# Deformable layer: the y offsets of two rows of taps are laid on all lanes by transfers, and three batches of tents are made per row of blocks

## The chip, the cores and the metric

The kernel runs on one core of a Trainium2 chip. The metric is the device time of one execution in microseconds; three runs of the kernel before gave 5567.96, 5574.5 and 5575.89 us, so the median is 5574.5 us. The core has five engines with a queue each, worked off in order: PE (matrix products; PEld is its loading of weights), DVE (elementwise and reductions), ACT (activations and copies), POOL and SP, which here only issues transfers. The transfers themselves run on 16 DMA engines.

## The reference, cut to what matters

Four layers follow one another on x of shape (4, 128, 128, 128), each with a group normalisation ahead of it and a residual sum behind it. The change touches only the first, a deformable 3x3 convolution:

```
offset = einsum('bchw,oc->bohw', x, w_off) + b_off          # 72 maps: 4 groups x 9 taps x {dy, dx}
py = dy + (ky - 1) + row ;  px = dx + (kx - 1) + column     # for each of the 9 taps (ky, kx)
y0, x0 = floor(py), floor(px)
val  = x[y0, x0]     * (1 - wy) * (1 - wx) + x[y0, x0 + 1]     * (1 - wy) * wx
     + x[y0 + 1, x0] * wy       * (1 - wx) + x[y0 + 1, x0 + 1] * wy       * wx
out  = relu(einsum('bgckhw,ogck->bohw', val, w_def))        # 9 taps x 128 channels -> 128 channels
x    = x + out
```

`wy` and `wx` are the fractions of py and px, and the 32 channels of a group share their offsets. A bilinear weight is a tent: max(0, 1 - |py - y|) * max(0, 1 - |px - x|) for each pixel (y, x).

## The kernel before

The layer is `deform_layer`. It assumes that no offset is larger than 1 (a flag `far` sends other inputs to `deform_general`), so that what a block of 3 rows by 4 columns of outputs needs lies in a window of 5 by 6 pixels. The 30 pixels of the window for each of 4 groups make 120 lanes (`LANES`). A sample is then a matrix product: the pixels of the window (`pixels`, 120 lanes x 128 channels, one such matrix for each of 33 column blocks) times the tents `m` (120 lanes x 27 x 4 columns), where a lane holds the weight of its own pixel for each of 9 taps and 3 rows.

The tents are made in three steps. `load_places` fetches the offsets of three rows of outputs (a "row of blocks") from DRAM (`offs`), where each offset is split into three bf16 parts and their positive parts (`parts`, 6 rows in each of 4 groups; with a row of ones that makes `KROWS` = 25). `spread_offsets` (line 498) multiplies them on PE with a constant table `spread`, which lays on each lane 1 - |offset - distance| in its row and clips it where the distance needs it. For one tap that takes three products for y (one per row, 130 columns) and four for x (one per column phase, 3 x 33 columns). Products of 25 rows use a quarter of the array each; two taps with y and x stand in the four quarters (partitions 0, 32, 64, 96) and are issued in turn. `tents` copies the y part out of PSUM on ACT (`ty`, line 508) and multiplies it with the x part on DVE (line 510). The PSUM tile `t_ps` has two buffers of two banks.

`sample` (line 521) multiplies pixels and tents for four column blocks, `keep_samples` (lines 531, 536) copies the result from PSUM to `v` on ACT, `convolved` (line 579) multiplies `v` with the weights of the 9 taps, and `finish` (line 552) adds the residual on DVE.

The order on each engine is the order of the code (`manual_schedule`). The main loop runs over 172 rows of blocks (43 in each of 4 images) and, inside, over `NG_X` = 8 groups of column blocks. In group i of row n it issues: the spreads of taps of row n + 1 that `DONE` asks for, the copy of the last group's samples, a piece of the convolution of row n - 1, the samples of group i, the tents of the spreads, up to six statistics of finished outputs (`count`), and one or two steps of the preparation of later rows (`step`). Five lists of taps (`SLOTS`, four pairs and a single) are spread per row, in groups 0, 2, 3, 5 and 6. `load_pixels` for row n + 1 is issued at the start of row n, `load_row` (which calls `load_places`) for row n + 2 in group 3.

Preparation is either `counted` (statistics of an image, 16 rows a chunk, for the group normalisation) or `prepared` (16 rows a job, four rows at a time): PE transposes (line 370), ACT scales (line 373), SP stores the pixel table; PE multiplies with `w_off` (line 385), DVE and POOL scale and shift it (lines 390, 393), ACT, POOL and DVE make the bf16 parts (lines 409 to 418) and the ranges for `far` (lines 412, 414), and SP stores the parts every eight rows (line 423). It keeps some 26 rows ahead of the samples.

In the last row of blocks of an image (`end`) a further output row is made with three extra tents (`me`) and samples (`ve`).

Of the kernel before, what the change touches and what calls it, by code (L numbers as in the profile page):

```python
# [49 lines left out]
SLOTS = [(0, 6), (1, 7), (2, 8), (3, 5), (4,)]  # L50
# [130 lines left out]
def deform_layer(tc, c, small, x, w_off, b_off, w_def, x1, tabs, offs):  # L181
# [13 lines left out]
    NB = RY * PADW  # L195
    with ExitStack() as ctx:
        wp = ctx.enter_context(tc.tile_pool(name="l0w", bufs=1))
        ps_g = ctx.enter_context(tc.tile_pool(name="l0ps_g", bufs=1, space=PSUM))
        ps_t = ctx.enter_context(tc.tile_pool(name="l0ps_t", bufs=2, space=PSUM))
# [4 lines left out]
        NPH = NPY + NPX  # L204
        keep = ctx.enter_context(tc.tile_pool(name="l0keep", bufs=2))
# [9 lines left out]
        places = [wp.tile([P, len(SLOTS), RY, OW], BF16, name=f"places_{i}") for i in range(3)]  # L215
        last = wp.tile([P, 3, 1, OW], BF16, name="places_last")
        pixels = [wp.tile([P, NXB + 1, P], F32, name=f"pixels_{i}") for i in range(2)]
        parts = wp.tile([2 * NL, NPART, 2 * RO * OW], BF16, name="parts")

        def rims():  # L220

            zero = two.tile([P, 2 * SX * P], F32, name="zero", tag="m")
            nc.vector.memset(zero, 0.0)
            zrow = zero[0 : NXB + 1]
            zoff = zero[0 : 2 * NL, 0 : NPART * OW].bitcast(BF16)
            zoff = zoff.rearrange("p (n l) -> p n l", n=NPART)
            for b in range(B):
# [14 lines left out]
                nc.scalar.dma_start(rows_[:, :, (S + 2) * OW :], zoff)  # L242

        def tables():

            awayi = two.tile([NG, NPH, LANES], I32, name="awayi", tag="x1c")
# [22 lines left out]
            for i, sign in enumerate((-1.0, 1.0, 1.0)):  # L269
                nc.gpsimd.memset(picks[:, i], sign)  # L270
# [17 lines left out]
            for t in (*pixels, parts):  # L288
                nc.gpsimd.memset(t, 0.0)
            yield  # L290
            picks16 = one.tile([NG, 3, P], BF16, name="picks16", tag="ve")
            nc.vector.tensor_copy(picks16, picks.rearrange("g k q r -> g k (q r)"))
            kinds = two.tile([NG, 3, NPH * LANES], BF16, name="kinds", tag="m")
# [10 lines left out]
            n = NPH * LANES // 3  # L304
            for h in range(3):
                if h % 2 == 0:
                    tp = ps_t.tile([P, 2, 512], F32, name="t_ps")
                at = slice(h * n, (h + 1) * n)
                for i in range(3):
                    nc.tensor.matmul(  # L310
                        tp[:, h % 2, 0:n], lhsT=picks16[:, i], rhs=kinds[:, i, at],
                        start=i == 0, stop=i == 2,
                    )
                nc.scalar.copy(to[:, at], tp[:, h % 2, 0:n])
# [43 lines left out]
        def prepared(b, y0):  # L358
# [6 lines left out]
            for h in range(0, RC, RO):  # L365
# [23 lines left out]
                off = one.tile([2 * NL, RO, S], F32, name="off")  # L389
# [8 lines left out]
                p0 = h % (2 * RO)  # L398
                at = slice(p0 * OW, (p0 + RO) * OW)

                def to(i):
                    return parts[:, i, at].rearrange("p (r c) -> p r c", c=OW)[:, :, 2 : S + 2]

                def high(t):
                    halves = t.rearrange("p r c -> p (r c)").bitcast(BF16)
                    return halves.rearrange("p (r c two) -> p r c two", r=RO, two=2)[:, :, :, 1]

                rest = one.tile([2 * NL, RO, S], F32, name="rest")
                nc.scalar.copy(to(0), high(off))
                nc.gpsimd.tensor_tensor(rest, off, high(off), ALU.subtract)  # L410
                flat = off.rearrange("p r c -> p (r c)")
                nc.vector.tensor_reduce(ranges[:, 0, n : n + 1], flat, AX.X, ALU.max)
                yield
                nc.vector.tensor_reduce(ranges[:, 1, n : n + 1], flat, AX.X, ALU.min)
                nc.scalar.copy(to(1), high(rest))
                nc.gpsimd.tensor_tensor(to(2), rest, high(rest), ALU.subtract)
                yield
                nc.vector.tensor_scalar(
                    parts[:, NSPLIT:, at], parts[:, 0:NSPLIT, at], 0.0, None, ALU.max
                )  # L420
                if p0:
                    r0 = y0 + h - p0 + 2
                    nc.sync.dma_start(
                        offs[b].rearrange("(p n) l -> p n l", n=NPART)[
                            :, :, r0 * OW : (r0 + 2 * RO) * OW
                        ],
                        parts,
                    )
                    ready[b] = y0 + h + RO
                    yield  # L430
                yield

        def shifted(b, d, k, n, row, count):

            ky, kx = divmod(k, 3)
            wide = (S + 4) * OW
            first = (d * NK + k) * NG * NPART
            whole = offs[b]
            return bass.AP(
                whole.tensor, whole.offset + first * wide + (row - ky + 2) * OW + 2 - kx,  # L440
                [[wide, NG * NPART], [NG * NPART * wide - 1, n], [1, count]],
            )

        def load_places(b, j):
            t = places[(b * NYB + j) % 3]
            for d in range(2):
                for q, slot, k, n in ((0, 0, 0, 3), (0, 3, 3, 2), (1, 0, 6, 3), (1, 3, 5, 1)):
                    p1 = 64 * d + 32 * q + 1
                    nc.sync.dma_start(
                        t[p1 : p1 + KROWS - 1, slot : slot + n].rearrange("p k r c -> p k (r c)"),  # L450
                        shifted(b, d, k, n, RY * j, RY * OW),
                    )
            if j + 1 == NYB:
                for d in range(2):
                    p1 = 64 * d + 33
                    nc.sync.dma_start(
# [1433 lines left out]
```

## Time and profile before

| | |
|---|---|
| median of three runs | 5574.5 us |
| the profiled execution | 5567.76 us |
| its span, first to last instruction | 5565.9 us |
| granted PE clock, mean | 0.971 |
| last sample of the layer (line 521) | between 3300 and 3400 us |
| spreads, line 498: instructions, PE busy | 10836, 520.0 us |
| samples, line 521: instructions, PE busy | 11352, 1462.3 us |
| convolution, line 579: instructions, PE busy | 5160, 1301.8 us |
| copies of y tents, line 508 (120x390): ACT busy, one | 685.0 us, 0.491 us |
| products of tents, line 510: DVE busy, one | 805.0 us, 0.557 us |
| copies of samples, line 531: ACT busy, one | 719.7 us, 0.523 us |

A line of a group in the profile names line, engine, operation, output<-inputs, their shapes and count, then busy time and mean duration of one, then how long the engine stood idle just before them and what ended that. A line of the timeline has the start in the span, the length, engine, line, operation and how many instructions it merges; what stands in brackets is the idle time before it and what released it. Matmul ends are modelled, so the distance from one start to the next says what a matmul costs. In the groups the fp32 products count twice.

### The profile page before, as it was taken

How to read it: one execution, taken by the hardware profiler on the slowest of the kernel's cores; microseconds unless marked ns; L12 is line 12 of the kernel's file. 1: busy time of each engine (PE TensorE's matmuls, PEld its weight loads, DVE VectorE, ACT ScalarE, POOL GpSimd, SP SyncE). 2: the span in 40 equal slices, each digit the busy share in tenths (PEclk: the TensorE clock that was granted, in tenths of full speed). 3: DMA queues.
4: the chain of work that ended last, by engine and by line, in shares of the span. 5: the costliest groups of instructions: out<-in, count | busy, mean ns of one | idle time of the engine just before them, and what ended most of it. 6: DMA issues, size and time to landing. Idle time of an engine off the chain costs nothing. (4 is left out here: it accounts for less than half of the span.)

```text
span 5565.9 us, 112097 instructions
## 1 busy us (share of the span) xinstructions
PE 5163.0 (93%) x42401; PEld 4438.1 (80%) x42401; DVE 3079.9 (55%) x10450; ACT 2721.1 (49%) x5802; POOL 787.0 (14%) x698
## 2 busy tenths in 40 slices
PE   2899999999999999999999989999989889898896
PEld 1778888888888888888888878999967768577686
DVE  6544444554444644444433337888876574764844
ACT  1345555445554455554544432333345475664755
POOL 2021111001111011111100002222210010110102
PEclk9899999999999999999999989999989999999999
DMA  4555555555555555554543423233232352642525
GB/s 142 146 129 137 128 136 122 127 118 135 133 131 119 131 112 137 129 141 113 124 78 76 76 56 91 91 107 103 91 100 92 97 195 80 207 147 82 203 95 169
DMA packets 1138394, 671.46 MB, mean 121 GB/s; under 512 B 737133, under 2 KB 1003566, under 8 KB 1121206
## 3 DMA queue, kind: packets, MB, share of 16 engines
q1 hardware_dynamic: 1127664, 657.77, 45.2%
q8 instruction: 338, 5.54, 0.4%
q10 hardware_dynamic: 10182, 6.43, 0.4%
q14 instruction: 210, 1.72, 0.1%
HBM read 382.88 MB, written 281.11 MB: 119 GB/s over the span
## 5 line engine op out<-in xcount | busy, mean ns | idle before, releaser
L510 DVE TENSOR_TENSOR m<-ty,t_ps 120x390 f32<-120x390 f32 x1548 | 805.0, 557 | 1497.2 <-ACT ty L508 1496.0
L521 PEld LDWEIGHTS v_ps<-m,pixels 120*128 120x128 f32 x11352 | 1436.1, 194 | 86.0 <-issue 8.7
L521 PE MATMUL v_ps<-m,pixels 120*128 120x108 f32 (+1 forms) x11352 | 1462.3, 273 | 3.6 <-ACT v L531 3.5
L531 ACT COPY v<-v_ps 128x432 f32<-128x432 f32 x1376 | 719.7, 523 | 1268.7 <-PE v_ps L521 1265.8
L579 PE MATMUL conv_ps<-v,wdef 128*128 128x128 f32 (+2 forms) x5160 | 1301.8, 378 | 6.5 <-DVE x1c L552 5.9
L579 PEld LDWEIGHTS conv_ps<-v,wdef 128*128 128x128 f32 x5160 | 812.8, 192 | 256.0 <-issue 21.7
L508 ACT COPY ty<-t_ps 120x390 f32<-120x390 f32 x1560 | 688.2, 489 | 176.9 <-PE t_ps L498 169.5
L498 PE MATMUL t_ps<-places,spread 25*120 25x99 bf16 (+1 forms) x10836 | 520.0, 259 | 62.1 <-DVE m L510 37.8
L498 PEld LDWEIGHTS <-spread 25*120 25x120 bf16 x10896 | 338.9, 136 | 224.5 <-issue 124.6
L1639 PEld LDWEIGHTS proj_ps<-wcat,X 128*128 128x128 f32 x4096 | 473.2, 192 | 19.1 <-issue 18.9
L393 POOL TENSOR_TENSOR off<-off,koff 72x512 f32<-72x512 f32 x128 | 162.1, 1266 | 2294.1 <-DVE off L390 2215.8
L1639 PE MATMUL proj_ps<-wcat,X 128*128 128x128 f32 x4096 | 481.3, 276 | 0.0
L1072 ACT ACTIVATE rowT<-x1T_ps,t_x,s_x 128x128 f32<-128x128 f32 x512 | 192.7, 457 | 366.4 <-PE x1T_ps L1065 342.8
L1085 PE MATMUL m_ps<-carry,w 128*128 128x172 f32 x2286 | 361.5, 311 | 0.0
L1646 DVE TENSOR_TENSOR L<-proj_ps,work 128x256 f32<-128x256 f32 x256 | 108.6, 424 | 430.0 <-ACT work L1643 429.9
L1085 PEld LDWEIGHTS m_ps<-carry,w 128*128 128x128 f32 x2286 | 345.5, 188 | 0.0
L1185 POOL TENSOR_TENSOR sum_h<-sum_h,x2c 128x512 f32<-128x512 f32 x128 | 163.2, 1275 | 1159.4 <-DVE x2c L1145 1159.4
L1736 POOL TENSOR_TENSOR gate<-normed,gate 128x512 f32<-128x512 f32 x128 | 163.4, 1276 | 1127.8 <-ACT normed L1735 867.2
L1643 ACT ACTIVATE work<-proj_ps 128x512 f32<-128x512 f32 x256 | 152.1, 598 | 293.2 <-PE proj_ps L1639 287.8
L1746 PE MATMUL out_ps<-outw,gate 128*128 128x128 f32 x1024 | 190.2, 288 | 30.3 <-POOL gate L1736 30.3
L1746 PEld LDWEIGHTS out_ps<-outw,gate 128*128 128x128 f32 x1024 | 162.9, 200 | 38.9 <-POOL gate L1736 38.9
L1449 PE MATMUL self_ps<-R,ws 128*128 128x512 f32 x256 | 147.3, 680 | 32.4 <-DVE X L1460 17.3
(237 smaller groups left out, 6499.6 us busy)
## 6 DMA issues: line engine op xcount, KB each, us to landing
pixels<-tab SPq DMA_DIRECT2D x688, 123.8 KB
xin<-in_x_dram SPq DMA_DIRECT2D x56, 1024.0 KB
off<-parts SPq DMA_DIRECT2D x64, 891.0 KB
tab<-rows SPq DMA_DIRECT2D x384, 128.0 KB
places<-off SPq DMA_DIRECT2D x688, 55.7 KB
x<-x1c SPq DMA_DIRECT2D x32, 1024.0 KB
x1rows<-x SPq DMA_DIRECT2D x128, 256.0 KB
x2T<-x2c SPq DMA_DIRECT2D x128, 256.0 KB
```

The lines of the kernel that those rows point to most:

```text
L498: nc.tensor.matmul(to, lhsT=spread[p0 : p0 + KROWS, ph, :], rhs=mov, start=True, stop=True,)
L508: nc.scalar.copy(ty[:, 0:n], tp[0:LANES, 0, 0:n])
L510: nc.vector.tensor_tensor(m, ty[:, 0:n].rearrange("p (r c) -> p r c", c=PADW), tx, ALU.mult)
L521: nc.tensor.matmul(vp[:, h * n : h * n + rows * w].rearrange("p (k c) -> p k c", c=w), lhsT=pix[0:LANES, xb, :], rhs=m[:, :, RX * xb : RX ...
L531: nc.scalar.copy(v[:, :, c0 : c0 + 4 * RX].rearrange("p k (h c) -> p k h c", c=RX), vp[:, 0 : 4 * n].rearrange("p (h k c) -> p k h c", h=4 ...
L579: nc.tensor.matmul(pc[:, at : at + r1 - r0, :], lhsT=wdef[:, 3 * ky + kx, :], rhs=v[:, k0 + kx, r0:r1, kx : kx + S], start=m == 0, stop=m ...
L1072: nc.scalar.activation(rt[:, b, :], px[:, b, :], AF.Identity, bias=t, scale=s)
L1085: nc.tensor.matmul(to, lhsT=wgt, rhs=src[:, :, at : at + n], start=i == 0, stop=i + 1 == len(todo),)
L1185: nc.gpsimd.tensor_tensor(sum_h, sum_h, x2c[:, :, i], add)
L1639: nc.tensor.matmul(pp[:, j], lhsT=X[:, j0 + j, :], rhs=wcat[:, cols], start=True, stop=True)
L1736: nc.gpsimd.tensor_tensor(gt, a, gt, ALU.mult)
L1746: nc.tensor.matmul(po[:, j], lhsT=a[:, j], rhs=outw, start=False, stop=True)
```

## The change

The y offsets of the taps in rows ky = 0 and 1 (six of nine) are no longer spread by PE. Their 24 maps are put first in `w_off` (`NLY`), stored in fp32 to a new DRAM tensor `offys` with the three column shifts of kx beside one another, and `same_on_lanes` describes a source that repeats the same 2 x 1188 numbers for each of the 30 lanes of a group; `load_places` loads them, one transfer per group, into `tent`, three buffers of 120 lanes x 3 ky x 3 rows x 3 kx x 132 columns. For each row of blocks ACT then takes |offset + distance of the lane| in place (`across`, one call per row, 120x792 each), DVE subtracts 1 and takes the minimum with 0 (`lowered`, 120x2376), which is the tent with its sign turned, and `tents` multiplies it with the x tents, whose sign is turned in the table `spread` (`picks`). The third row of taps, ky = 2, still has its y offsets spread.

A batch now holds one kx: x offsets for three ky in three quarters of the array and y offsets for ky = 2 in the fourth, fifteen products into one `t_ps` tile of four banks, of which there is one buffer. Three batches are spread per row of blocks, in groups 2, 4 and 6; `across` stands in groups 0 (one row) and 1 (two rows), `lowered` in group 1, and `load_row` moves from group 3 to group 1. In `tents` two DVE products replace one per tap: one of 792 elements for ky = 0 and 1, one of 396 for ky = 2. `places` has two buffers instead of three and three slots instead of five. `offs` holds 48 maps instead of 72. `prepared` keeps the offsets in `wide`, stores them from there in three transfers for each four rows, and stores the bf16 parts every four rows instead of every eight. `m` is `tent` itself, so its order of taps, and that of `v`, becomes ky, row, kx.

```diff
+NLY = 2 * 3 * NG
...
-        ps_t = ctx.enter_context(tc.tile_pool(name="l0ps_t", bufs=2, space=PSUM))
+        ps_t = ctx.enter_context(tc.tile_pool(name="l0ps_t", bufs=1, space=PSUM))
...
-        places = [wp.tile([P, len(SLOTS), RY, OW], BF16, name=f"places_{i}") for i in range(3)]
+        lane_y = wp.tile([LANES, RY], F32, name="lane_y")
+        places = [wp.tile([P, KS, RY, OW], BF16, name=f"places_{i}") for i in range(2)]
+        wide = wp.tile([2 * NL, RO, OW + 2], F32, name="offwide")
+        tent = [wp.tile([LANES, KS, RY, KS, OW], F32, name=f"tent_{i}") for i in range(3)]
...
-            for i, sign in enumerate((-1.0, 1.0, 1.0)):
+            for i, sign in enumerate((1.0, -1.0, -1.0)):
...
+                for kx in range(KS):
+                    nc.sync.dma_start(
+                        offys[b][:, r0 : r0 + RO, kx, :],
+                        wide[2 * NG * kx : 2 * NG * (kx + 1), :, 2 - kx : 2 - kx + OW],
+                    )
...
+                nc.sync.dma_start(
+                    offs[b].rearrange("(p n) l -> p n l", n=NPART)[:, :, r0 * OW : (r0 + RO) * OW],
+                    parts[NLY:],
+                )
+                ready[b] = y0 + h + RO
...
+        def same_on_lanes(b, g, row):
+
+            whole = offys[b]
+            return bass.AP(
+                whole.tensor,
+                whole.offset + (g * (S + 4) + row + 2) * KS * OW,
+                [[0, NS], [(NG * (S + 4) - 1) * KS * OW, KS - 1], [1, RY * KS * OW]],
+            )
+
         def load_places(b, j):
-            t = places[(b * NYB + j) % 3]
...
+            t = places[(b * NYB + j) % 2]
+            y = tent[(b * NYB + j) % 3]
+            from_ = [(X0 + KS * NG * NPART * ky, ky) for ky in range(KS)] + [(0, KS - 1)]
+            for q, (first, ky) in enumerate(from_):
+                nc.sync.dma_start(
+                    y[q * NS : (q + 1) * NS, 0 : KS - 1].rearrange("p i r k c -> p i (r k c)"),
+                    same_on_lanes(b, q, RY * j),
+                )
+                nc.sync.dma_start(
+                    t[32 * q + 1 : 32 * q + KROWS].rearrange("p k r c -> p k (r c)"),
+                    shifted(b, first, ky, RY * j, RY * OW),
+                )
...
+        def spread_offsets(src, rows, taps):
+
+            tp = ps_t.tile([P, KS + 1, 512], F32, name="t_ps")
+            ph0 = 0 if rows == RY else RY
+            for i in range(NPX):
+                cs = slice(i, OW, RX)
+                for q in (*taps, KS):
+                    at = slice(32 * q, 32 * q + KROWS)
+                    to = tp[0:LANES, q, 0 : rows * OW].rearrange("p (r c) -> p r c", c=OW)
+                    if q < KS:
                         nc.tensor.matmul(
-                            to, lhsT=spread[p0 : p0 + KROWS, ph, :], rhs=mov,
+                            to[:, :, cs], lhsT=spread[at, NPY + i, :], rhs=src[at, :, cs],
                             start=True, stop=True,
                         )
...
+                    elif i < rows:
+                        nc.tensor.matmul(
+                            to[:, i], lhsT=spread[at, ph0 + i, :], rhs=src[at, i],
+                            start=True, stop=True,
+                        )
+            return tp
+
+        def across(n, r):
+            t = tent[n % 3][:, 0 : KS - 1, r].rearrange("p k x c -> p k (x c)")
+            nc.scalar.activation(t, t, AF.Abs, bias=lane_y[:, r : r + 1])
+
+        def lowered(n):
+            t = tent[n % 3][:, 0 : KS - 1]
+            nc.vector.tensor_scalar(t, t, 1.0, 0.0, ALU.subtract, ALU.min)
+
+        def tents(tp, m, loaded, rows):
+
+            n = rows * OW
+            ty = two.tile([LANES, RY * OW], F32, name="ty")
+            nc.scalar.copy(ty[:, 0:n], tp[0:LANES, KS, 0:n])
+            tx = tp[0:LANES, 0:KS, 0:n].rearrange("p k (r c) -> p k r c", c=OW)
+            if loaded is not None:
+                nc.vector.tensor_tensor(loaded, loaded, tx[:, 0 : KS - 1], ALU.mult)
             nc.vector.tensor_tensor(
-                m, ty[:, 0:n].rearrange("p (r c) -> p r c", c=PADW), tx, ALU.mult
+                m, ty[:, 0:n].rearrange("p (r c) -> p r c", c=OW), tx[:, KS - 1], ALU.mult
             )
...
             for i in range(NG_X):
-                if i == 3:
+                if i == 1:
                     load_row(n + 2)
-                todo = advance(NB_ * (n + 1) + DONE[i])
+                kx = i // 2 - 1
+                batch = more and i in (2, 4, 6)
+                if batch:
+                    tp = spread_row(n + 1, kx)
                 if vps is not None:
                     keep_samples(*vps)
                 next(convs, None)
                 vps = sample(m, pix, i, NK * RY), vk, i, NK * RY
-                multiply(todo)
-                if end and i in (1, 4, 7):
-
-                    kx = i // 3
-                    tents(spread_offsets(last, kx, (1,), 1)[0], me[:, kx : kx + 1, :], 1)
+                if more and i < 2:
+                    for r in range(i, 2 * i + 1):
+                        across(n + 1, r)
+                if more and i == 1:
+                    lowered(n + 1)
+                if batch:
+                    multiply(n + 1, kx, tp)
+                if end and i in (3, 5, 7):
+
+                    kx = (i - 3) // 2
+                    tents(spread_offsets(last[:, kx], 1, (KS - 1,)), me[:, kx], None, 1)
                 count(6)
```

## The prediction

> **What bounds the kernel now.** I read the page first: busy shares, then the slices, for where one engine is saturated.
>
> ```profile
> span 5565.9 us, 112097 instructions
> ...
> PE 5163.0 (93%) x42401; PEld 4438.1 (80%) x42401; DVE 3079.9 (55%) x10450; ACT 2721.1 (49%) x5802; POOL 787.0 (14%) x698
> ...
> PE   2899999999999999999999989999989889898896
> ...
> DMA  4555555555555555554543423233232352642525
> ```
>
> Each digit is 139 us. The deformable layer fills the first 24 slices, and after two of them PE is at 9: only what shortens PE's own queue, or stops it, counts there. DMA is at 5 while the offsets are still prepared (to about 2780 us) and 4, then less, after. The windows view (PE, PEld, DVE, ACT, POOL, clock, DMA share, GB/s) says this of two stretches of the layer:
>
> ```profile
> 1000.00:2000.00 1000.00, 986.88 (x9055) 835.20 (x9055) 516.21 (x1704) 508.88 (x1112) 120.25 (x108) 0.98 0.55 126
> 2900.00:3000.00 100.00, 100.00 (x954) 86.12 (x953) 35.29 (x92) 47.95 (x109) 0.00 (x0) 1.00 0.40 73
> ```
>
> PE has no gap; DVE and ACT are half idle. I call the second stretch, without preparation, the light one. PE's timeline there, the spreads (L498) and what follows three of them (start, length):
>
> ```profile
> 2925.77 0.56 PE L498 MATMUL t_ps<-places,spread 25*120 25x130 bf16 x14
> 2926.26 1.56 PE L579 MATMUL conv_ps<-v,wdef 128*128 128x256 f32 x6
> ...
> 2929.97 0.56 PE L498 MATMUL t_ps<-places,spread 25*120 25x130 bf16 x14
> ...
> 2931.98 0.73 PE L498 MATMUL t_ps<-places,spread 25*120 25x130 bf16 x14
> 2932.64 0.71 PE L579 MATMUL conv_ps<-v,wdef 128*128 128x128 f32 x4
> ...
> 2936.35 0.56 PE L498 MATMUL t_ps<-places,spread 25*120 25x130 bf16 x14
> ...
> 2938.99 0.55 PE L498 MATMUL t_ps<-places,spread 25*120 25x130 bf16 x7
> 2939.47 1.13 PE L579 MATMUL conv_ps<-v,wdef 128*128 128x256 f32 x4
> ...
> 2942.49 0.56 PE L498 MATMUL t_ps<-places,spread 25*120 25x130 bf16 x14
> ```
>
> One row of blocks takes 2942.49 - 2925.77 = 16.72 us, of which five spread batches hold PE, start to next start, 0.49, 0.49, 0.66, 0.49 and 0.48 = 2.61 us. Seven matmuls cost as much as fourteen: a batch costs its longest lane group (3 or 4 matmuls), not its count. While offsets are prepared a row takes about 18.0 us (a spread at 2649.44, its like at 2667.45). ACT and DVE beside it:
>
> ```profile
> 2912.01 0.53 ACT L531 COPY v<-v_ps 128x432 f32<-128x432 f32 x1 [1.45 <-PE v_ps L521]
> ...
> 2913.84 0.87 ACT L508 COPY ty<-t_ps 120x390 f32<-120x390 f32 x2
> ...
> 2914.36 1.03 DVE L510 TENSOR_TENSOR m<-ty,t_ps 120x390 f32<-120x390 f32 x2 [3.12 <-ACT ty L508]
> ```
>
> Two ACT copies of 0.49 last 0.87, two DVE products of 0.557 last 1.03: back to back, one hides 0.11 or 0.08 of the other. Rows for the new operations (busy, mean ns) and for the transfers:
>
> ```profile
> L510 DVE TENSOR_TENSOR m<-ty,t_ps 120x390 f32<-120x390 f32 x1548 | 805.0, 557 | 1497.2 <-ACT ty L508 1496.0
> ...
> L1559 DVE TENSOR_SCALAR X<-X,s,t 128x512 f32<-128x512 f32 x96 | 51.6, 538 | 1.0 <-DMA x3d<-X 1.0
> ```
> ```profile
> L1467 ACT ACTIVATE junk<-X,lessb 128x512 f32<-128x512 f32 x128 | 91.9, 719 | 51.6 <-DVE X L1460 51.6
> ...
> L1561 ACT ACTIVATE X<-X,t,s 128x512 f32<-128x512 f32 x32 | 25.7, 816 | 1.2 <-DMA x3d<-X 1.2
> ```
> ```profile
> DMA packets 678372, 284.77 MB, mean 129 GB/s; under 512 B 498805, under 2 KB 647050, under 8 KB 669946
> ```
>
> The last line is of 300 to 2500 us.
>
> **1. PE's saving.** Five batches become three of fifteen matmuls, again at most four in a lane group: 3 x 0.49 = 1.47 us. Saved 2.61 - 1.47 = 1.14 us a row, x 172 rows = 196 us, all on PE's path. PE's other waits for L510 (18 us between 300 and 2500 by the view of waits) take a new form; I put 20 us to the credit.
>
> **2. ACT.** Six copies of 0.49 go (2.9 us a row); three Abs of 120x792 come. L1467 (bias, 512 elements) is 719 ns; ACT's slope is about 0.83 ns an element (512 against 128 elements: 816 and 484 ns), so 719 + 280 x 0.83 = 0.95 us, between 0.86 (a plain copy of 512, L415, 0.623) and 1.06 (L1561). 2.9 against 2.9: ACT stays half idle, but two Abs stand in a row in group 1. [...]
>
> **3. DVE.** Nine products of 0.557 (5.0 us a row) become three of 396 (0.56), three of 792 (0.557 + 402 x 1.02 ns = 0.97) and one subtract-and-min of 2376. The latter's slope from TENSOR_SCALAR rows (L1559 538 at 512, L1599 351 at 127) is 0.486 ns, so 1.31 to 1.44; 1.38 taken. 6.0 us a row; DVE has room.
>
> **4. The new wait, which decides.** t_ps has one buffer instead of two, so the spread of group 4 waits until the products of group 2's batch are read out. The chain that ends there begins where sample 0 ends, 0.29 us after PE turns to group 1: keep_samples 0.42, two Abs 0.84 + 0.95, hand-over 0.03, subtract-and-min 1.38, product 0.97 - 0.08 + 0.08 (it waits for a DVE signal), product 0.56, hand-over 0.05: 5.47 us. PE's own work from there to group 4, taken from the light timeline without group 3's batch, is 4.9. The wait is 0.55 us (0.3 to 0.85 from the bounds of 2 and 3). While rows are prepared, PE has its transposes and offset matmuls (0.6 and 1.0 us every eight steps) in that stretch, which eat the wait in about half of the alignments, while DVE's reductions of 0.67 behind the subtract-and-min lengthen it in two of eight: mean 0.35, plus 0.1 for x1 statistics. Where the statistics of the next image run (some 21 rows; eight bn_stats, 1.0 us, in most steps) it is 1.2. Sum: 110 x 0.45 + 21 x 1.2 + 41 x 0.65 = 101 us back. Groups 4 to 6 have 5 us for a chain of 2.6 and wait for nothing. Queued behind PE's wait are the convolution and sample 4, so all of it is lost.
>
> **5. Transfers.** A row now loads 4 x 30 x 2 x 4752 B = 1.14 MB of y offsets in place of 0.11 MB of places; offset stores go from one per eight rows to eight (2 + 6), about 0.2 MB less. Rates: 388 GB/s in slices of the first dense loads (2.9 us a row) against 129 GB/s at a 55.5% share, 232 (4.9 us). DMA's time a row rises from 0.555 x 18.0 = 10.0 to 13 or 15 us of some 17.4: no bound on the mean, but later stores and x loads queue behind, since each transfer on SP waits for the eighth before it (so the order of the built program). Loads have seven groups, some 14 us, before Abs needs them. SP itself issues some 2.6 more transfers a row, 0.4 to 0.9 us each, with idle stretches of 5 us a row around it. Late x loads stop DVE's statistics or PE's transposes, late stores of offwide or parts stop DVE or ACT. Bounds: 0 (all in the 4 to 6 us in which DMA idles per row at 600 to 640 us) and 100 us (24 statistics chunks and 32 prepared ones, 1.8 us each). I take 30, nearer the idle rows. [...]
>
> **6. Ends and start.** In four last rows the extra spread shares the one buffer: 2 us each, less the like before, +6. At the start two loads of 1.14 MB stand before the first pixels, and three batches run in turn: +10 (0 to 20). Convolution and sampling read other strides at equal counts: 0, and without cover if they should differ, since PE has no gap.
>
> **Sum**: -196 - 20 + 101 + 30 + 6 + 10 = -69 us on the profiled execution's 5567.8 (1.9 above its span): 5499. The median of the three runs is 6.7 above that execution: 5505.
>
> **Rivals.**
> (a) The wait is hidden: Abs at 0.86, subtract-and-min at 1.31, and preparation's PE work covers the rest; some 25 us come back for 101, transfers cost 5: 5405. Against it: the light chain exceeds PE's 4.9 even then.
> (b) Slower by the single buffer: the subtract-and-min runs at the products' 1.02 ns an element, 2.6 us, so the wait grows by 1.2 to about 1.8 us a row, 310 us: 5715. It decides from 1 us a row on ((216 - 46) / 172). Against it: all f32 TENSOR_SCALAR rows out of SBUF have half the slope.
> (c) Slower by transfers: thirty lanes read the same 4752 bytes at once, which no row of this trace does. If a load takes two to three times the 4.9 us, DMA exceeds the row's 17.4 us while offsets are prepared, and Abs, at ACT's head, holds back keep_samples and so PE: 2 us x 131 rows = 260, 5735; at 1.3 us a row, 5645. It decides from 0.8 us a row on. Against it: idle stretches; for it: DMA already at 0.9 in bursts.
> (d) The parts cancel: wait 0.85 and transfers 50: within 0.2% of before.
>
> **How the numbers follow.** A measurement of this kernel tells 0.2%, 11 us, from no change. Forecast 0.43 (its own range 5440 to 5560), (a) 0.10, (b) 0.12, (c) 0.28, (d) 0.07. Faster 0.53, same 0.07, slower 0.40. The range leaves out half of (a) below and the worst of (b) and (c) above: 5425 to 5690.
>
> **What would show it.** t_ps batches of fifteen, three a row, 0.49 apart from what follows; a light row of 16.1 us; PE waiting for DVE before the second batch, 0.5 us, and hardly before the others; Abs near 0.95, subtract-and-min near 1.4; DMA share near 0.7 up to 2700 us. Wrong if Abs waits for its transfers by tens of us in all, if the subtract-and-min takes over 2 us, or if a batch of fifteen costs more than 0.6.

## The result, and the profile after

The changed kernel takes 5658.4 us (median of 4 runs, 5647.0 to 5668.7) against 5571.2 for the kernel before on the same chip: 1.0155 times as long, with a 95% interval of 1.0129 to 1.0182. It is slower by 87 us, where 5505 and "faster" were forecast.

The page of the profiled execution of after (5666.4 us): busy shares, then some of the 40 slices (142 us each).

```profile
span 5664.7 us, 106382 instructions
...
PE 5031.3 (89%) x39311; PEld 4344.7 (77%) x39311; DVE 3231.4 (57%) x10107; ACT 2715.4 (48%) x5286; POOL 775.0 (14%) x702
...
PE   2689899999999899999999997999988889899896
...
DMA  5778788778887888887777752233322252542525
```

PE has 132 us less work than before and yet the layer ends later: the last sample of a full row starts at 3383 us, before it was 3291. Behind the layer nothing moved (2282 us from there to the end, before 2275). DMA stood at 4 to 5 while offsets were prepared and stands at 7 to 8.

The windows view of after (PE, PEld, DVE, ACT, POOL, clock, DMA share, GB/s), first over the two stretches shown of before, then over the end of the layer, then over 30 us that are read below:

```profile
1000.00:2000.00 1000.00, 916.13 (x7760) 782.62 (x7760) 529.14 (x1474) 485.78 (x912) 111.50 (x102) 0.95 0.82 170
2900.00:3000.00 100.00, 90.90 (x743) 75.51 (x743) 47.16 (x93) 50.03 (x93) 16.41 (x16) 0.93 0.80 162
3100.00:3200.00 100.00, 95.68 (x889) 83.80 (x888) 43.70 (x84) 51.24 (x96) 0.00 (x0) 1.00 0.76 142
...
1540.00:1556.00 16.00, 13.22 (x111) 11.06 (x109) 6.24 (x20) 4.83 (x9) 2.64 (x3) 1.00 0.79 183
1556.00:1570.00 14.00, 11.39 (x61) 9.06 (x62) 7.74 (x27) 6.30 (x12) 0.61 (x1) 0.63 0.93 179
```

While offsets are prepared PE works 916 us of 1000 (before 987), at a clock of 0.95 (before 0.98). The stretch at 2900 now still holds preparation (POOL at work); the light stretch lies at 3100, and there PE is idle 4%, at full clock.

The new operations have the durations that were forecast (groups of the page: busy, mean ns, idle before and its releaser):

```profile
L545 DVE TENSOR_TENSOR tent<-tent,t_ps 120x792 f32<-120x792 f32 x516 | 502.6, 974 | 597.9 <-ACT ty L542 589.0
L536 DVE TENSOR_SCALAR tent<-tent 120x2376 f32<-120x2376 f32 x172 | 241.6, 1404 | 765.9 <-ACT tent L532 703.2
L532 ACT ACTIVATE tent<-tent,lane_y 120x792 f32<-120x792 f32 x516 | 474.8, 954 | 101.8 <-DMA tent<-offy 37.5
...
L546 DVE TENSOR_TENSOR tent<-ty,t_ps 120x396 f32<-120x396 f32 x516 | 288.0, 558 | 0.0
```

So the work is as priced; what is new is waiting. Waits of PE in after (engine, line, releaser: us, times, longest) from the second row of blocks to the last; in before all of them came to 58 us between 130 and 3266 us, here to 284:

```profile
PE t_ps L519 <- DVE tent L546: 138.9, 133, 7.9
PE conv_ps L615 <- DVE x1c L588: 43.7, 62, 6.9
PE v_ps L557 <- ACT v L567: 34.8, 25, 7.1
PE img_ps L392 <- DMA xin<-in_x_dram: 22.7, 8, 6.0
```

The first line is the forecast wait for the single `t_ps`. Its longest, 7.9 us, is not: the chain of step 4 is 5.5 us long and most of it is covered. One stop of PE shows what else is at work. First the timeline of SP's queue (start, length):

```profile
1540.01 0.43 SPq L480 DMA_DIRECT2D tent<-offy  x1
1540.49 0.36 SPq L484 DMA_DIRECT2D places<-off  x1
...
1542.56 0.37 SPq L480 DMA_DIRECT2D tent<-offy  x1
1543.10 0.29 SPq L484 DMA_DIRECT2D places<-off  x1
1550.72 0.60 SPq L447 DMA_DIRECT2D off<-parts  x1
1551.37 0.60 SPq L598 DMA_DIRECT2D x<-x1c  x1
```

Then the timeline of all engines, ACT and PE out of it (in brackets the idle time before, and its releaser):

```profile
1550.35 0.96 ACT L532 ACTIVATE tent<-tent,lane_y 120x792 f32<-120x792 f32 x1 [1.17 <-DMA tent<-offy]
...
1551.05 1.04 PE L557 MATMUL v_ps<-tent,pixels 120*128 120x108 f32 x8
...
1555.52 0.62 ACT L430 COPY parts<-offwide 72x512 bf16<-72x512 bf16 x1 [4.21 <-DMA off<-parts]
...
1556.61 1.14 PE L557 MATMUL v_ps<-tent,pixels 120*128 120x108 f32 x8 [3.39 <-ACT v L567]
...
1559.23 2.04 PE L557 MATMUL v_ps<-tent,pixels 120*128 120x108 f32 x8 [0.84 <-ACT v L567]
...
1566.02 1.88 PE L557 MATMUL v_ps<-tent,pixels 120*128 120x108 f32 x8
```

SP issues the row's four y loads and four `places` loads, eight transfers in 3.4 us, and then stands still for 7.3 us. The next transfer is the store of `parts` into the DRAM tensor `offs` (`off` in the profile). By the semaphores in the trace it waits for the four `places` loads, which read that tensor. The last of them, issued at 1543.10 behind 1.14 MB of y offsets, lands at 1550.53, and the store goes out at once. (The program counts SP's transfers on eight semaphores in turn, 100 and 102 to 108 in the trace, so each also waits for the eighth before it. That one, the first y load, had landed at 1544.52: here it was not what held the store.) The values of the store had been finished by DVE at 1537.4 (L444); it goes out 13 us late. `parts` has one buffer, so ACT's next write to it (L430) waits 4.21 us for the store to land. ACT also empties `v_ps`, so PE stops 3.39 us for ACT. And when PE goes on, two groups of eight sample matmuls take 2.04 and 1.88 us in place of 1.04: the mean granted clock of those 14 us is 0.63 (the window above); it is 0.50 from 1557.9 to 1568.1 us and 1.00 on either side. In these 10.2 us PE stops twice more (0.84 and 1.17 us).

### The profile page after: what moved, and what is told of

It is laid out like the page before. It is cut to its first block, busy times and chain, and to the rows that moved or that the text cites. A ratio compares the mean times of both kernels' runs of the same rounds, so it can differ in the third digit from the quotient of the medians.

```text
span 5664.7 us, 106382 instructions
## 1 busy us (share of the span) xinstructions
PE 5031.3 (89%) x39311; PEld 4344.7 (77%) x39311; DVE 3231.4 (57%) x10107; ACT 2715.4 (48%) x5286; POOL 775.0 (14%) x702
## 5 line engine op out<-in xcount | busy, mean ns | idle before, releaser
L557 PEld LDWEIGHTS v_ps<-tent,pixels 120*128 120x128 f32 x11352 | 1466.9, 197 | 157.8 <-ACT v L567 44.9
L557 PE MATMUL v_ps<-tent,pixels 120*128 120x108 f32 (+1 forms) x11352 | 1491.2, 278 | 54.3 <-ACT v L567 36.4
L545 DVE TENSOR_TENSOR tent<-tent,t_ps 120x792 f32<-120x792 f32 x516 | 502.6, 974 | 597.9 <-ACT ty L542 589.0
L536 DVE TENSOR_SCALAR tent<-tent 120x2376 f32<-120x2376 f32 x172 | 241.6, 1404 | 765.9 <-ACT tent L532 703.2
L532 ACT ACTIVATE tent<-tent,lane_y 120x792 f32<-120x792 f32 x516 | 474.8, 954 | 101.8 <-DMA tent<-offy 37.5
L415 POOL TENSOR_TENSOR offwide<-offwide,koff 72x512 f32<-72x512 f32 x128 | 150.4, 1175 | 2496.4 <-DVE offwide L412 1953.6
L1683 PEld LDWEIGHTS proj_ps<-wcat,X 128*128 128x128 f32 x4096 | 472.2, 192 | 20.1 <-issue 19.9
L519 PE MATMUL t_ps<-places,spread 25*120 25x99 bf16 x6192 | 299.2, 284 | 162.1 <-DVE tent L546 146.3
L519 PEld LDWEIGHTS <-spread 25*120 25x120 bf16 x6240 | 194.8, 146 | 267.0 <-DVE tent L546 179.2
L542 ACT COPY ty<-t_ps 120x396 f32<-120x396 f32 (+1 forms) x528 | 255.6, 484 | 233.0 <-PE t_ps L519 203.8
L546 DVE TENSOR_TENSOR tent<-ty,t_ps 120x396 f32<-120x396 f32 x516 | 288.0, 558 | 0.0
```

Source lines behind the costliest of these rows:

```text
L519: nc.tensor.matmul(to[:, :, cs], lhsT=spread[at, NPY + i, :], rhs=src[at, :, cs], start=True, stop=True,)
L532: nc.scalar.activation(t, t, AF.Abs, bias=lane_y[:, r : r + 1])
L536: nc.vector.tensor_scalar(t, t, 1.0, 0.0, ALU.subtract, ALU.min)
L542: nc.scalar.copy(ty[:, 0:n], tp[0:LANES, KS, 0:n])
L545: nc.vector.tensor_tensor(loaded, loaded, tx[:, 0 : KS - 1], ALU.mult)
L546: nc.vector.tensor_tensor(m, ty[:, 0:n].rearrange("p (r c) -> p r c", c=OW), tx[:, KS - 1], ALU.mult)
```

## The experiments

Times are medians; the kernel before, run beside them, gave 5568.0 to 5574.5. The interval of each ratio is about 0.2% to either side, 10 us. Where engines stand and wait is added up from the views of waits, over the layer (some 130 to 3420 us) unless another stretch is given.

**What the loads cost, and what in them.**

```
 for q, (first, ky) in enumerate(from_):
+    if b == 0 and j < 3:
         nc.sync.dma_start(y[...], same_on_lanes(b, q, RY * j))
```


> The changed kernel, but the y offsets are transferred to the lanes only for the first three rows of blocks; every later row works on what is left in its tent buffer, so the tents of ky = 0 and 1 are not those of their row and 1.14 MB a row is not moved. All instructions of PE, ACT, DVE and POOL stay. Theory T (transfers): what turned a gain into a loss is that the loads take DMA some 6.5 us a row and make everything behind them late; then this kernel is faster than the kernel before, near 5500 us (ratio 0.985 to 0.993), with a DMA share near 0.5 while offsets are prepared and no row of ACT waiting for the tent transfers. Theory W (the single buffer of t_ps in itself): PE's wait for DVE before the second batch stays at its 136 us and the time stays at 5600 us or more (ratio 1.006 or more).

Measured: 5488.2 (ratio 0.985, 0.984 to 0.987). The loads cost 170 us, not 30; the rest of the forecast, 5505 - 30 = 5475, is 13 us off. PE's wait for `t_ps` is not theirs for the most part: it is 116 us here, 139 in after. Next, the same number of transfers with a ninth (e6: 132 of the 1188 values of each piece, not of 594, as its expectation says) or half of the bytes (e9: 594 of 1188, the first half of the piece):

```
+n = RY * KS * OW if b == 0 and j < 3 else OW            # e9: else RY * KS * OW // 2
-y[q * NS : ..., 0 : KS - 1].rearrange(...), same_on_lanes(b, q, RY * j)
+y[q * NS : ..., 0 : KS - 1].rearrange(...)[:, :, 0:n], same_on_lanes(b, q, RY * j, n)
```


> Left out: after the first three rows of blocks each load of the y tents brings only its first row of one pixel column (OW of 594 values for each tap) into the 30 lanes; the tents are otherwise made of what the buffer holds, so the values are wrong. As many transfers as before, in the same places of SP's queue, with a ninth or less of the bytes. If the number of transfers and their slots in the queue is what costs: 5600 or more. If the bytes and the time that they take is what costs: 5485 to 5520, near the kernel without these loads (5488).

> Left out: after the first three rows of blocks each load of the y tents brings half of its bytes (the first three of six pixel columns of each tap), the rest of the tent is what the buffer holds, so the values are wrong. As many transfers as in the changed kernel. If the cost of the loads is proportional to their bytes: half of the 170 us, 5570 to 5580. If it sets in where the DMA engines come near their limit (share 0.82, now about 0.7): well under half, 5500 to 5540.

Measured: 5490.6 and 5508.5. The number of transfers costs nothing by itself (2 us); half of the bytes cost 20 us, the other half 150. The price grows faster than the bytes. So does the wait seen above, of the store of `parts` for the `places` loads: SP stands still for it, between 300 and 2500 us, for 29 us without the y loads, 24 with a ninth, 70 with half and 146 with all of the bytes; ACT waits for the landing of these stores 13, 12, 23 and 74 us.

Two readings of why the bytes are dear were tried. In e3 each lane reads bytes of its own (out of `x`) in place of thirty lanes reading the same; in e4 the lanes are numbered 4 x pixel + group, so that the thirty lanes of a load lie four apart, over all 120 (the loads of the pixels and the constant tables go with them):

```
-[[0, NS], [(NG * (S + 4) - 1) * KS * OW, KS - 1], [1, RY * KS * OW]]          # e3
+[[2500, NS], [1250, KS - 1], [1, RY * KS * OW]]
...
-y[q * NS : (q + 1) * NS, 0 : KS - 1]                                           # e4
+y[q:LANES:NG, 0 : KS - 1]
```


> The changed kernel with another source for the four y transfers of a row: each of the 30 lanes reads its own 2 x 4752 bytes of the input image, not the same bytes 30 times; destination, sizes and number of transfers are unchanged. The tents of ky = 0 and 1 are therefore not those of the reference. Theory H (30 lanes that read the same bytes slow the load): DMA share while offsets are prepared falls from 0.82 to about 0.70, the time to 5580 us or less. Theory P (30 neighbouring lanes as destination slow the load, or any load of this size costs this): share 0.80 to 0.84 and time within 15 us of the changed kernel's 5658.

> The changed kernel with the lanes in another order: lane = 4 x pixel + group in place of 30 x group + pixel. Each y transfer and each pixel transfer then writes 30 lanes four apart, over all 120, in place of 30 neighbours; bytes, packets and all work on the engines are unchanged. Theory P (neighbouring lanes as destination slow the load): DMA share while offsets are prepared falls from 0.82 to 0.70 or less and the time to 5580 us or less. Theory H (same bytes read 30 times): share and time as in the changed kernel, within 15 us of 5658.

Measured: 5683.7 and 5633.3. Reading the same bytes is not the cause, since other bytes are no faster. Interleaved lanes take the DMA share from 0.81 to 0.68 at the same rate (168 and 170 GB/s, over the layer), but only 25 us off the time, and beside other edits, below, they cost 21. The share is no measure of the price.

**The single buffer.** e2 moves the batches one group later, which gives the chain one group more:

```
-batch = more and i in (2, 4, 6)
+batch = more and i in (3, 5, 7)
```


> The changed kernel with its three batches in groups 3, 5 and 7 in place of 2, 4 and 6 (the extra tents of an image's last row move to groups 2, 4 and 6). By the durations now measured (Abs 0.954, subtract-and-min 1.404, product 0.974 us) the first product then ends 0.8 us after its old time, but the next batch is due 2.1 us later, so the wait for the buffer goes. Theory W: PE's wait for DVE before the batches falls from 136 us to under 40 and the time falls by 100 us or more, to 5560 or less. Theory T: the waits come from late transfers, the time falls by 40 us at most, to some 5620, as one more group of slack hides part of the lateness.

Measured: 5621.1, 37 us less. PE's wait for `t_ps` falls from 139 to 50 us, while its wait for ACT's `v` rises from 36 to 84: here, where transfers are late, a stop that ended in one place began in another.

**Another queue.** The y loads from GpSimd's queue (e5: `nc.gpsimd.dma_start` in place of `nc.sync.dma_start`), and one at a time, at the end of groups 1 to 4, from ScalarE's (e7) and from SP's (e10):

```
-for q, (first, ky) in enumerate(from_):
-    nc.sync.dma_start(y[...], same_on_lanes(b, q, RY * j))
+if i in (1, 2, 3, 4):                # at the end of group i
+    load_y(n + 2, i - 1)             # one y load; e7: nc.scalar, e10: nc.sync
```


> The loads of the y tents are issued from GpSimd's queue (it has almost no work in the layer) and no longer stand in SP's; bytes, places and times of the loads stay. Theory Q (what costs is that other transfers stand behind these loads in SP's queue, and late transfers stop ACT, DVE and PE): most of the 170 us that the loads cost comes back, 5490 to 5560, and ACT's wait for the stores of parts (74 us in the changed kernel) falls under 30. Theory B (the 16 DMA engines have not the time: share 0.82): the bytes compete as before whoever issues them, 5630 to 5670. If GpSimd issues slowly or is late itself (its sums of the offsets stand in the same queue), the sums come late and the time is above 5660.

> The four loads of the y tents of a row of blocks are issued one at a time, at the end of groups 1 to 4, from ScalarE's queue, in place of all four in group 1 from SP's. Bytes and places as in the changed kernel. Theory Q (order: what stands behind these loads in SP's queue is late): SP's stores and x loads are early again, ACT pays four issues of about 0.6 us a row in groups with room: 5500 to 5580, and ACT's wait for the stores of parts falls from 74 us to under 30. Theory B (the DMA engines lack the time, whoever issues): 5630 to 5670, the waits for parts, xin and offwide stay.

> As the run with ScalarE's queue, one load at the end of each of groups 1 to 4, but from SP's queue as in the changed kernel. If the burst of four loads (1.14 MB at once) ahead of the stores is what makes them late: 5560 to 5610. If it is that they share SP's queue at all, or that the DMA engines lack the time: 5640 to 5670.

Measured: 5813.0, 5744.5 and 5622.5. Both other queues are worse, but neither run shows that a queue of its own is no use. In e5 GpSimd holds each load until PE has read the buffer (594 us of waits between 300 and 2500), and its own sums of the offsets, which everything else needs, stand behind that. e7 does not separate the loads from SP: by the semaphores in its trace the program counts ScalarE's loads on the same eight semaphores as SP's transfers, so that SP's transfers wait for them: 464 us between 300 and 2500, where the y loads in SP's own queue had cost it 176. The largest part stands before the `places` loads:

```profile
SPq L488 <- DMA tent<-offy: 200.9, 82, 6.3
```

The theory that it is SP's queue that must be freed made the wrong forecast for both, but neither run puts it to a clean test. e10, from SP's queue, gains 36 us by the place of the loads alone.

**The place in time.** The whole burst one group earlier (e13), and one load at the end of each of groups 0 to 3 (e14), both with nothing else changed:

```
-if i == 1:                           # e13 and e14
+if i == 0:
     load_row(n + 2)
...
+if i < 4:                            # e14 alone: the y loads, no longer in load_row
+    load_y(n + 2, i)
```


> One edit to the changed kernel: the row's loads (all of load_row) stand in group 0 in place of group 1. If landing late at ACT's Abs is the cause: 20 to 50 us less, 5610 to 5640. If the burst ahead of the stores is the cause, it only moves: 5650 to 5670.

> One load at the end of each of groups 0 to 3 from SP's queue, nothing else (batches in groups 2, 4, 6 and lanes in blocks as in the changed kernel). If place in time and queue is the cause by itself: 5622 less the 65 us that the move by a group was worth beside the other edits, 5550 to 5570. If it needs the slack of the other two: 5600 to 5625.

Measured: 5764.9 and 5576.4. The same bytes, from the same queue, to the same buffers, differ by 189 us according to where they stand. e13 was expected to gain or to do nothing, and lost 107 us. What stands behind the burst there is the load of `xres`; SP waits before it for y loads (117 us, 108 times, at most 1.8 us, between 300 and 2500; mostly for the eighth transfer before it), and it then lands behind them. DVE's addition waits for it (106 us, 42 times), and PE's convolution for that (94 us, 44 in after). The stores of `parts` wait for the `places` loads here too, and ACT stands 127 us for their landing, 74 in after. In e14 82 of the 170 us come back. The waits of SP's queue between 300 and 2500 us, first after, then e14:

```profile
...
SPq L447 <- DMA places<-off: 145.5, 59, 7.1
SPq L434 <- DMA tent<-offy: 83.7, 83, 1.7
...
SPq L484 <- DMA off<-parts: 46.6, 16, 3.4
...
SPq L400 <- DMA tent<-offy: 39.5, 48, 1.9
```
```profile
...
SPq L447 <- DMA places<-off: 25.0, 45, 2.7
...
SPq L504 <- DMA xin<-in_x_dram: 13.9, 5, 5.8
...
SPq L479 <- DMA pixels<-tab: 12.6, 19, 1.7
```

The longest wait of the first line, 7.1 us, is the standstill read above. Where the four `places` loads stand apart from the y loads, as in e14, the store hardly waits for them. All SP waits for transfers add up to 415 us in after, 427 in e13, 144 in e10, 88 in e14, and 101 in before.

**Together.** Four kernels with batches in groups 3, 5 and 7 and the y loads one at a time:

| run | lanes | y loads | us |
|---|---|---|---|
| e8 | interleaved | ScalarE's queue, groups 1 to 4 | 5569.6 |
| e11 | interleaved | SP, groups 1 to 4 | 5571.9 |
| e12 | interleaved | SP, groups 0 to 3 | 5507.1 |
| e15 | in blocks, as in the change | SP, groups 0 to 3 | 5486.5 |

> Three edits together: the batches in groups 3, 5 and 7 (37 us alone), lanes interleaved (25 us alone), and the y loads one at a time from ScalarE's queue in groups 1 to 4. Theory Q: 5430 to 5520, below the kernel before (5571). Theory B: the first two alone, 5590 to 5610.

> Batches in groups 3, 5 and 7 (37 us alone), lanes interleaved (25 us alone) and the y loads one at a time at the end of groups 1 to 4 from SP's queue (36 us alone). If the three causes add: 5658 - 98 = 5560. If each of the last two shortens the same waits behind the loads: 5580 to 5600. If a row with slack in both PE and the queue loses its waits altogether (light rows at 15.3 us, prepared ones at about 17): 5480 to 5530, faster than before by over 1%.

> As the run with the three edits, but the loads stand one group earlier (groups 0 to 3), so that they have one group, about 2 us, more before ACT's Abs. If loads that land late at Abs are what is left (ACT waited 112 us for them with the loads in groups 1 to 4 alone): 20 to 50 us below the run with groups 1 to 4. If the lateness only moves to the stores and x loads: within 10 us of it.

> Batches in groups 3, 5, 7 and loads in groups 0 to 3, lanes in blocks of 30 as in the changed kernel. If the higher DMA share of 30 neighbouring lanes matters where waits are few: 5525 to 5550 against 5507 with lanes interleaved. If it is no cause: 5500 to 5515.

e12 against e11: one group earlier (the `places` loads too) is worth 65 us, more than the 20 to 50 expected, and ACT's wait for the y loads falls from 164 to 64 us, the reason that was expected. e15 against e12: the interleaved lanes cost 21 us, against both readings given. e15 leaves nothing out and is faster than both kernels: 0.985 of before (0.984 to 0.987). e16 takes e12 and moves the load of the pixels, for whose buffer SP waited 170 us between 300 and 2500, from ahead of group 0 to group 2:

```
-pixel_tiles[n + 1] = load_pixels(*blocks[n + 1])    # ahead of group 0
+if more and i == 2:
+    pixel_tiles[n + 1] = load_pixels(*blocks[n + 1])
```


> The kernel with three edits and the loads in groups 0 to 3 (5507), and the pixels of the next row loaded in group 2 instead of ahead of group 0, when their buffer has long been read: SP no longer waits for PE (170 us between 300 and 2500) with the loads and stores behind it. If the order in SP's queue is what makes transfers late: 5460 to 5490. If the DMA engines' time is: 5500 to 5515. Above 5515 if the pixels then land late.

Measured: 5511.4, as without it. That wait of SP is gone, but at the `places` loads, first in line now, SP waits 131 us for stores of `parts` and 124 for PE (from 19 us, all its waits for transfers rise to 165). So the run does not tell whether the wait was in anybody's way. Last, e15 without the loads (`if i < 4 and n == 0`):

> Left out: the loads of the y tents after the first three rows of blocks (as in the first run), in the kernel with batches in groups 3, 5, 7 and loads in groups 0 to 3; the values are wrong. If place and grouping are nearly the whole price of the loads: 5440 to 5475. If the transfers still cost some 90 us through the DMA engines' time: 5380 to 5420. The difference to the first run (5488) is the single buffer's price without transfers: forecast 101, so 5387.

Measured: 5378.3. So the loads still cost 108 us at their best place found, and without them the batches in groups 2, 4 and 6 cost 5488.2 - 5378.3 = 110 us more than in 3, 5 and 7: the price of the single buffer, with the convolution's waits that come with it (below).

**Where the time lies.** From the timelines of DVE, the starts of the subtract-and-min (one a row of blocks) give the time of a row; the windows view from the second row's to the last row's gives PE's busy and idle time. PE's instructions are the same 25,000 in all.

| kernel | rows 2 to 20, us each | 21 to 126 | 161 to 170 (light) | PE busy | idle | clock | DMA share |
|---|---|---|---|---|---|---|---|
| after | 22.0 | 18.85 | 16.04 | 2941 | 285 | 0.95 | 0.81 |
| e13, burst in group 0 | 24.2 | 19.27 | 16.19 | 2965 | 362 | 0.94 | 0.80 |
| e14, groups 0 to 3 | 21.1 | 18.31 | 16.04 | 2903 | 231 | 0.96 | 0.77 |
| e1, no loads | 20.0 | 17.76 | 16.05 | 2863 | 184 | 0.98 | 0.52 |
| e15, groups 3, 5, 7 and 0 to 3 | 21.5 | 17.84 | 15.25 | 2889 | 166 | 0.96 | 0.79 |
| e17, e15 without loads | 19.9 | 17.15 | 15.25 | 2844 | 95 | 0.98 | 0.54 |

Two things are to be read here. In light rows the loads cost nothing, in after as in e15: all of their price lies where offsets are prepared, beside the stores and the x loads. And the price has two halves: after less e1 is 101 us of waiting and 78 us of the same matmuls taking longer at a lower clock (2863 x 0.98 / 0.95 would be 2953). e15 less e17: 71 and 45. The transfers alone did not lower the clock in the light stretch of after: with a DMA share of 0.76, it was 1.00. The single buffer, e1 less e17, whose stops are short: 89 and 19.

## Why the prediction was wrong, step by step

**Step 5 (transfers) failed.** It put 30 us on them, between 0 and 100; they cost 170. Part of the mechanism was there ("later stores and x loads queue behind"), and so was the list of who would wait. What failed is threefold. The bound of 100 us counted 56 chunks at 1.8 us each, where every prepared row was exposed: 1.09 us on each of the rows 21 to 126, 2.0 on the first twenty. The reason given, "each transfer on SP waits for the eighth before it", is not what held up the stores of `parts`: these wait for the `places` loads, which read the tensor that they write and which now land behind 1.14 MB of y offsets (146 us of SP between 300 and 2500, 29 without the loads); the step has no such wait. And it reasoned with means, "no bound on the mean", where the burst made what follows it late (the last `places` load, read above, landed 7.4 us after its issue). By the step's own DMA times, 2.9 to 4.9 us a row, the share should rise to 13 to 15 us of a row; measured is 0.82 of 18.9, 15.5. Against e1 (0.54 of 17.8, 9.6; both shares between 300 and 2500 us) the loads took 5.9 us of the DMA engines a row, more than its upper 4.9. That the place and the grouping of the loads decide about half of the price is shown (5576, 5658 and 5765 us at equal bytes). How much of the 82 us that e14 regains comes from the stores' wait is not shown: no run takes that wait away by itself.

What remains after the place has been mended, 88 us from e14 to e1 or 108 from e15 to e17, is not settled. That the first half of the bytes costs 20 us and the second 150 would fit DMA engines near their limit in the prepared rows, but also the stores that wait for `places` loads behind the burst; that the share fell by a sixth in e4 with little gain speaks against the share as its measure. No run separates these.

**A term was missing: PE's clock.** The prediction priced each wait at its length. The waits that the loads bring, long stops among them, cost two thirds to three quarters of their length again (78 on 101, 45 on 71), the short ones of the single buffer a fifth (19 on 89).

**Step 1 (PE's saving) was too small.** A batch of fifteen costs 0.49 us to what follows, as forecast. But the matmuls beside a batch are longer too. PE's timeline of a light row in e15, where nothing waits:

```profile
2960.73 1.04 PE L561 MATMUL v_ps<-tent,pixels 120*128 120x108 f32 x8
2961.70 0.30 PE L523 MATMUL t_ps<-places,spread 25*120 25x99 bf16 x3
...
2962.19 0.71 PE L619 MATMUL conv_ps<-v,wdef 128*128 128x128 f32 x4
2962.74 1.04 PE L561 MATMUL v_ps<-tent,pixels 120*128 120x108 f32 x8
...
2967.57 1.04 PE L561 MATMUL v_ps<-tent,pixels 120*128 120x108 f32 x8
2968.44 1.05 PE L619 MATMUL conv_ps<-v,wdef 128*128 128x256 f32 x4
...
2974.18 0.63 PE L619 MATMUL conv_ps<-v,wdef 128*128 128x128 f32 x4
2974.64 1.04 PE L561 MATMUL v_ps<-tent,pixels 120*128 120x108 f32 x8
...
2976.95 0.30 PE L523 MATMUL t_ps<-places,spread 25*120 25x99 bf16 x3
```

The row takes 2976.95 - 2961.70 = 15.25 us, against 16.72 before: 1.47 saved, not 1.14. From a sample's start to a batch it is 0.97 us, to a convolution 0.87 to 0.88; a convolution of 4 x 128 takes 0.55 to the next start behind a batch, 0.46 elsewhere. A batch is thus dearer by about 0.09 on either side, and two batches fewer save 0.36 more than their own time: 0.33 x 172 = 57 us. Both pairs stand in before's light row too: from a sample to a batch 2929.00 to 2929.97, to a convolution 2927.66 to 2928.54; the convolution of 4 x 128 behind a batch 2930.46 to 2931.01, elsewhere 2928.54 to 2929.00.

**Step 2** holds: Abs 0.954 us against 0.95. (The rows that it names, 816 and 484 ns, give a slope of 0.86 and not 0.83 ns an element, so 0.96.) **Step 3** holds: 0.974, 0.558 and 1.404 against 0.97, 0.56 and 1.38. So rival (b) is out.

**Step 4 (the wait for the single buffer)** was sized well in sum: 116 us by PE's wait for `t_ps` in e1, 110 by e1 and e17, against 101. (The terms of its chain add up to 5.49 us, not 5.47; that changes nothing.) Part of it balances: a light row waits 16.05 - 15.25 = 0.80 us, near the upper bound of 0.85, where 0.55 was taken, probably because the batch's true price also shortens PE's cover; with step 1's larger saving the light row still comes to 16.05 against the 16.1 forecast. What it missed is "Groups 4 to 6 ... wait for nothing": the third batch's products stand ahead of the convolution's result on DVE, and PE's convolution waits for `x1c` 62 times, 44 us (31 in e1, without loads). In e15, with the batch in group 7, that is 15.

**Step 6** can't be told from the rest: the first rows cost 20.0 us even without loads, and the loads' 2.0 us more a row there are in the 170.

**The sum.** Without loads and without the wait, the steps give 5571.2 - 196 - 20 + 6 + 10 = 5371; e17 has 5378. With the wait, 5475 forecast, 5488 measured. That they meet so closely is luck in part: the 57 us that step 1 left out are not in the forecast, and costs of about the same size are missing from it too: PE still stands idle for 95 us in e17, for 57 in before, where 20 us of waits were credited. Of the miss, 5505 to 5658, 140 us are the transfers and the clock that falls with them.

**The rivals.** (c) had the right side and, at 1.3 us on 131 rows, the time: 5645, by luck. Its reason, thirty lanes reading the same bytes, is refuted by e3, and its place, Abs at ACT's head, holds 67 us of ACT's waits for loads and for stores of `offwide`, against 74 for the stores of `parts`. (a) would have needed both the later batches and loads that cost nothing: e17's 5378 is below it, e15's 5486 is what can be had of it here. (d) was not seen in the change, though e14, e8 and e11 come out there.

## What to carry to other kernels

The loads here, which nobody needs soon, were not free when they were issued in a burst ahead of small stores (170 us): look which later transfer must wait for one of such a burst, by its turn in the queue or because it writes what one of them reads, and what it holds up (here the stores behind the `places` loads, then one buffer of `parts`, then ACT, then PE). Before giving up such a change, move the loads: one per group and a group earlier was worth 82 us, and with the batches a group later the change became 1.5% faster than the kernel before. Where PE is the bound, do not price its waits at their length alone: those that the loads brought here cost 1.6 to 1.8 times their length, with the lower clock behind them.

## What was not expected of the hardware

- What followed a stop ran slower: behind PE's stop of 3.39 us in after the same eight matmuls took 2.04 and 1.88 us in place of 1.04, with a granted clock of 0.50 over 10.2 us; the idle 0.8 us of each light row left it at 1.00 (3100 to 3200 us).
- The DMA share differed with the lanes that the loads wrote: 0.81 for thirty neighbouring lanes (after), 0.68 for thirty lanes four apart (e4), at 168 and 170 GB/s over the layer; e15 and e12 differ likewise, 0.79 and 0.71 at 177 GB/s each. The lower share did not make the kernel faster there.
